# Spectral norms by chains of squarings: a scale at every third of 20 squarings instead of every second of 22, and two traces at the end

## The chip, the cores and the metric

The kernel runs on one core of one Trainium2 chip. The metric is the device time of one execution in microseconds (us). Before the change it is 1932.47 us, the median of 3 runs (1932.23 to 1932.93). The profiled execution spans 1930.8 us.

## The reference

The input x has 8 images of 512 channels and 1024 pixels, in f32. Four layers follow each other. Only the first has to do with the change:

```
f = relu(batchnorm(Wf x));  g = relu(batchnorm(Wg x));  h = Wh x     (64 channels each)
z = f^T g                                  per image, 1024 x 1024, of rank 64 at most
sigma = largest singular value of z        (S[:, 0] of an SVD)
x = Wv (z / sigma applied to h) + x
```

Layer 1 is a group norm with softmax attention over 1024 pixels, layer 2 an attention with 128 channels, layer 3 a product with the signs of a 512 x 512 weight matrix and an elementwise end.

The square of sigma is the largest eigenvalue of the 64 x 64 matrix (f f^T)(g g^T). The kernel never forms z. It squares this small matrix again and again, takes traces on the way to keep the numbers in range, and gets the logarithm of the eigenvalue as a weighted sum of the logarithms of the traces.

## The kernel before

**Layout.** Two images share one 128 x 128 matrix with two 64 x 64 blocks on the diagonal, so 8 images make 4 chains of squarings. For pair `j`, the tile `gm[j]` holds f f^T, g g^T and the product of h and g; it is made by `gram` (L1309, matmuls at L1312), from transposed tiles that `turn` (L1113, transposes at L1117) writes. `mask2` has ones in the two diagonal blocks; a matmul of it with a column sums that column within each image.

**A chain.** `chain(j, split)` (L995) is a generator: each `yield` hands control back, so that other work can be written between two steps. `products` (L1005) does one squaring: one matmul for the power and one for its transpose (L1008, L1009), both from the tile `cur`, which holds the two. `evict` (L1012) copies the results from PSUM to a new `cur`: with no scale, on ScalarE (L1022), or with `split` the first half on VectorE (L1024); with a scale on VectorE (L1030), or with `split` the second half on ScalarE (L1026). `diagonal` (L1033) multiplies with the identity and sums along each row (L1036, L1037), `total` (L1040) adds these row sums within an image by a matmul with one column (L1042) and copies the result to `tr` (L1043). The first trace is taken from f f^T and g g^T and divides the first product. Then come NSTEP = 11 rounds of two squarings. The second of a round is scaled by a power of the reciprocal of the trace taken a round earlier. After the last round there is a last trace; a logarithm (L1080), a weighted sum with the constants `quarters`, and an exponential (L1083) give 1 / sigma, which scales the matrix for the output (L1087). That makes 24 steps, 23 pairs of products and 12 totals in a chain.

**The first chain** (images 6 and 7, `split` on) stands in a block in which TensorE runs in the order of the program text (L1425). After each step of the chain the loop at L1428 writes a number of pieces of other work, taken from the generator `filler` (L1395): products of weights (L1265), Gram matrices (L1312), transposes (L1117), bias products (L1290), the scaling of z (L1173 to L1180). It also writes one `relu` (L1338), which runs on ScalarE. After the chain, `entering(0)` (L850) makes pv from the scaled matrix (L282) and the input of layer 1 of the first image (L403). What is left of `filler` comes after that.

**The other three chains** (`behind`, L1104) run inside the work of the first images: `fast` (L868) calls `chore(2)` after the pieces of the scores, the value weights and the values of layer 1, and every second call advances the chain by one step. The order of instructions there is set by the scheduler from the program text. Each engine then runs its instructions in that order. `entering` (L850) needs the chain of its pair to be finished.

**Buffers.** In the first part PSUM has two tiles of two banks (`wide`) and four of one bank (`bank`); products, totals, turns and bias products share the four. Later there are eight of one bank.

Of the kernel before, what the change touches and what calls it, by code (L numbers as in the profile page):

```python
# [8 lines left out]
F32 = mybir.dt.float32  # L9
F16 = mybir.dt.float16  # L10
I32 = mybir.dt.int32
AF = mybir.ActivationFunctionType
ALU = mybir.AluOpType
# [3 lines left out]
P = 128  # L17
# [47 lines left out]

NSTEP = 11

# [12 lines left out]
def kernel(  # L84
# [17 lines left out]
    nc = tc.nc  # L102
    mm = nc.tensor.matmul

    const = ctx.enter_context(tc.tile_pool(name="const", bufs=1))
# [4 lines left out]
    spin = ctx.enter_context(tc.tile_pool(name="spin", bufs=2))  # L110
# [10 lines left out]
    def bank():  # L121
        return psum["bank"].tile([P, HF], F32, tag="bank", name="bank")
# [17 lines left out]
    def half(i):  # L140
        return bass.ts(i, HF)

    def side(i):

        return slice(i * MID, (i + 1) * MID)
# [21 lines left out]
    ident = const.tile([P, P], F32, tag="ident", name="ident")  # L167
    make_identity(nc, ident)

    def block_ones(size, value, name):  # L170

        n = P // size
        member = const.tile([P, n], F32, tag=name + "_m", name=name + "_m")
        nc.vector.tensor_reduce(
            member, ident.rearrange("p (g j) -> p g j", j=size), AX.X, ALU.add
        )
        t = const.tile([P, n, size], F32, tag=name, name=name)
        nc.vector.tensor_scalar(
            t, member.unsqueeze(2).to_broadcast([P, n, size]), value, None, ALU.mult
        )  # L180
        return t.rearrange("p g j -> p (g j)")

    mask2 = block_ones(MID, 1.0, "mask2")
# [24 lines left out]
    minus_half = const.tile([P, CC], F32, tag="minus_half", name="minus_half")  # L208
    nc.gpsimd.memset(minus_half, -0.5)

    quarters = const.tile([P, NSTEP], F32, tag="quarters", name="quarters")
    for s in range(NSTEP):
        nc.gpsimd.memset(quarters[:, s : s + 1], 0.25**s)

    def vec(name):
        return ct[:, COL[name] : COL[name] + CC]
# [633 lines left out]
    def entering(n):  # L850

        b = order[n]
        f = load_f(b)

        def steps():
            while b // 2 not in ready:
                next(behind)
            if b % 2 == 0:
                for i in (b, b + 1):
                    pvs[i] = weights0(i)  # L860
            yield from enter(resident[b], f, pvs.pop(b))

        return steps()
# [131 lines left out]
    def chain(j, split):  # L995

        ff, gg, gh = (gm[j][:, i, :] for i in range(3))
        tr = spin.tile([P, NSTEP + 1], F32, tag="tr", name="tr")  # L1000

        def column(name):
            return spin.tile([P, 1], F32, tag=name, name=name)

        def products(a, at):  # L1005
            ps = [bank()] if not split else [bank(), bank()]
            pa, pb = ps[0][:, 0:P], ps[-1][:, 0:P] if split else ps[0][:, P : 2 * P]
            mm(out=pa, lhsT=at, rhs=a, start=True, stop=True)  # L1008
            mm(out=pb, lhsT=a, rhs=at, start=True, stop=True)  # L1009
            return ps[0], pa, pb  # L1010

        def evict(got, r=None, again=None, full=None):  # L1012

            both, pa, pb = got
            cur = spin.tile([P, 2, P], F32, tag="cur", name="cur")
            parts = [(cur[:, 0], pa), (cur[:, 1], pb)]
            if not split:
                parts = [(cur.rearrange("p i c -> p (i c)"), both[:, 0 : 2 * P])]
            for i, (dst, ps) in enumerate(parts):
                if r is None:  # L1020
                    if i or not split:
                        nc.scalar.copy(dst, ps)  # L1022
                    else:
                        nc.vector.tensor_copy(dst, ps)  # L1024
                elif i:
                    nc.scalar.activation(dst, ps, AF.Copy, scale=full)  # L1026
                elif again is None:
                    nc.vector.tensor_scalar(dst, ps, r, None, ALU.mult)
                else:
                    nc.vector.tensor_scalar(dst, ps, r, again, ALU.mult, ALU.mult)  # L1030
            return cur

        def diagonal(u, v):  # L1033
            d = spin.tile([P, P], F32, tag="diag", name="diag", bufs=1)
            t = column("tj")
            nc.vector.tensor_tensor(d, u, v, ALU.mult)  # L1036
            nc.vector.tensor_reduce(t, d, AX.X, ALU.add)  # L1037
            return t

        def total(t, s):  # L1040
            ps = bank()
            mm(out=ps[:, 0:1], lhsT=mask2, rhs=t, start=True, stop=True)  # L1042
            nc.vector.tensor_copy(tr[:, s : s + 1], ps[:, 0:1])  # L1043

        t = diagonal(ff, gg)
        got = products(gg, ff)
        total(t, 0)
        r = column("r")
        nc.vector.reciprocal(r, tr[:, 0:1])
        cur = evict(got, r, None, r)  # L1050
        yield

        root, half_ = column("root"), column("half_")
        nc.gpsimd.tensor_tensor(root, tr[:, 0:1], minus_half[:, 0:1], ALU.pow)
        nc.vector.tensor_tensor(half_, root, root, ALU.mult)
        nc.vector.tensor_tensor(half_, half_, tr[:, 0:1], ALU.mult)
        nc.vector.tensor_scalar(half_, half_, -0.5, 1.5, ALU.mult, ALU.add)
        nc.vector.tensor_tensor(root, root, half_, ALU.mult)
        t = None
        for s in range(1, NSTEP + 1):  # L1060
            cur = evict(products(cur[:, 0], cur[:, 1]))
            yield
            got = products(cur[:, 0], cur[:, 1])
            if t is None:
                cur = evict(got)
            else:
                total(t, s - 1)
                r, r2, r4 = column("r"), column("r2"), column("r4")
                nc.vector.reciprocal(r, tr[:, s - 1 : s])
                nc.vector.tensor_tensor(r2, r, r, ALU.mult)  # L1070
                if split:
                    nc.vector.tensor_tensor(r4, r2, r2, ALU.mult)
                cur = evict(got, r2, r2, r4)
            t = diagonal(cur[:, 0], ident)
            yield
        total(t, NSTEP)

        ln = spin.tile([P, NSTEP], F32, tag="ln", name="ln")
        rsig = column("rsig")
        nc.scalar.activation(ln, tr[:, 1:], AF.Ln)  # L1080
        nc.vector.tensor_tensor(ln, ln, quarters, ALU.mult)
        nc.vector.tensor_reduce(rsig, ln, AX.X, ALU.add)
        nc.scalar.activation(rsig, rsig, AF.Exp, scale=-0.125)  # L1083
        nc.vector.tensor_tensor(rsig, rsig, root, ALU.mult)
        for i in range(2):
            rr = side(i)
            nc.vector.tensor_scalar(  # L1087
                ff[rr, :].rearrange("p (i c) -> p i c", c=MID),
                gh[rr, rr].unsqueeze(1).to_broadcast([MID, 2, MID]),
                rsig[rr, :],  # L1090
                None,
                ALU.mult,
            )
        ready.add(j)
        yield
# [4 lines left out]
    def chains():  # L1100
        for j in rest:
            yield from chain(j, False)
# [109 lines left out]
    last = None  # L1212
    for b in range(B):
# [9 lines left out]
        def products(i, cc):  # L1223
            for h in range(NH):
                mm(  # L1225
                    out=banks[i][side(h), :],
                    lhsT=w0[i][:, cc, :],
                    rhs=xt[:, cc, half(h)],
                    start=cc == 0,
                    stop=cc == CC - 1,  # L1230
                )
# [22 lines left out]
        last = b, hraw  # L1254
# [83 lines left out]
    def relu(b, i):  # L1338
        t = (fs, gs)[i][b]
        nc.scalar.activation(t, t, AF.Relu, bias=bi0[:, i : i + 1], scale=sc0[:, i : i + 1])  # L1340
        if i == 0:
            nc.sync.dma_start(out=f_dram[b], in_=t)
# [10 lines left out]
    ps = bank()  # L1353
# [5 lines left out]
    ps = bank()  # L1359
# [65 lines left out]
    with tc.manual_schedule(engines={mybir.EngineType.PE}):  # L1425
        steps = entering(0)
        for k, _ in enumerate(chain(jl, True)):
            for _ in range(2 - k % 2 if k <= 2 * NSTEP else 4):  # L1428
                next(todo, None)
            for args in (next(relus, None),):  # L1430
                if args:
                    relu(*args)
        for k in range(CC + 2):
            next(steps)
            for _ in range(3 if k < CC else 5):
                next(todo, None)
        for _ in todo:
            pass
# [9 lines left out]
    with ExitStack() as main:  # L1448
# [5 lines left out]
        got = []  # L1454
# [177 lines left out]
```

## Time and profile before

| what | value |
|---|---|
| time, median of 3 | 1932.47 us |
| span of the profiled run | 1930.8 us |
| TensorE busy (matmuls) | 1906.6 us, 99% |
| weight loads of TensorE | 987.4 us, 51% |
| VectorE busy | 1158.2 us, 60% |
| ScalarE busy | 507.7 us, 26% |
| GpSimd busy | 229.7 us, 12% |
| granted TensorE clock | 0.998 |

PE in the profile is TensorE's matmuls, PEld its weight loads, DVE is VectorE, ACT ScalarE, POOL GpSimd. A line of the timeline gives the start and length in us, the engine, the line of the program, the operation, output<-inputs, and the number of records; in brackets, how long the engine stood idle before, and what ended that. One f32 matmul leaves two records of each kind. A length includes the time that a matmul takes to run through the array, so lengths of neighbours overlap, and what a matmul costs among others is read from start to start. The first chain begins at 114.1 us (matmuls that read gm). The other three lie between 225 and 758 us.

### The profile page before, as it was taken

How to read it: one execution, taken by the hardware profiler on the slowest of the kernel's cores; microseconds unless marked ns; L12 is line 12 of the kernel's file. 1: busy time of each engine (PE TensorE's matmuls, PEld its weight loads, DVE VectorE, ACT ScalarE, POOL GpSimd, SP SyncE). 2: the span in 40 equal slices, each digit the busy share in tenths (PEclk: the TensorE clock that was granted, in tenths of full speed). 3: DMA queues.
4: the chain of work that ended last, by engine and by line, in shares of the span. 5: the costliest groups of instructions: out<-in, count | busy, mean ns of one | idle time of the engine just before them, and what ended most of it. 6: DMA issues, size and time to landing. Idle time of an engine off the chain costs nothing.

```text
span 1930.8 us, 16673 instructions
## 1 busy us (share of the span) xinstructions
PE 1906.6 (99%) x6230; PEld 987.4 (51%) x6230; DVE 1158.2 (60%) x1875; ACT 507.7 (26%) x807; POOL 229.7 (12%) x178
## 2 busy tenths in 40 slices
PE   9999999999999999999999999999999999999997
PEld 4367456544655447454555446544645455544653
DVE  3256677448764687537754676348663775466647
ACT  2141222135222332025212331034202421143114
POOL 0000001200111001300121011201120011201121
PEclk9999999999999999999999999999999999999999
DMA  8420000002000120002000120002000200010001
GB/s 319 154 77 7 1 6 12 1 11 87 17 1 0 33 71 12 1 11 87 17 1 1 33 71 11 1 11 87 11 0 1 84 15 11 0 33 22 11 1 46
DMA packets 27784, 66.47 MB, mean 34 GB/s; under 512 B 4272, under 2 KB 5424, under 8 KB 27056
## 3 DMA queue, kind: packets, MB, share of 16 engines
q1 hardware_dynamic: 26768, 64.90, 10.0%
q8 instruction: 51, 0.84, 0.2%
q10 hardware_dynamic: 864, 0.43, 0.1%
q14 instruction: 37, 0.30, 0.1%
q0 software_dynamic: 64, 0.00, 0.0%
HBM read 38.51 MB, written 18.87 MB: 30 GB/s over the span
## 4 chain that ended last, share of the span: by engine, by line
PE 91%; DVE 7%; ACT 1%; issue 1%; DMA 0%; POOL 0%; DVEq 0%; ACTq 0%
PE bank L380 41%; PE bank L547 20%; PE bank L937 6%; PE bank L796 6%; PE bank L1225 4%; PE bank L648 3%; PE bank L403 2%; PE bank L665 2%; PE bank L1008 1%; PE wide L1265 1%; DVE both L739 1%; DVE both L709 1%; PE bank L1009 1%; PE wide L1312 1%; PE bank L688 1%; PE bank L817 1%
## 5 line engine op out<-in xcount | busy, mean ns | idle before, releaser
L547 PE MATMUL bank<-e,vt 128*128 128x512 f32 x768 | 334.0, 593 | 0.0
L547 PEld LDWEIGHTS bank<-e,vt 128*128 128x128 f32 x768 | 145.0, 190 | 175.4 <-issue 173.2
L380 PE MATMUL bank<-ut,h 128*128 128x512 f32 x384 | 181.3, 596 | 0.0
L337 DVE TENSOR_TENSOR e<-bank,e 128x512 f32<-128x512 f32 x128 | 87.6, 684 | 61.1 <-PE bank L380 60.3
L380 PE MATMUL bank<-us,hs 128*128 128x512 f32 x256 | 122.1, 599 | 1.3 <-DVE us L309 0.5
L380 PEld LDWEIGHTS bank<-ut,h 128*128 128x128 f32 x384 | 71.5, 190 | 85.8 <-issue 83.6
L937 PE MATMUL bank<-e,tpg 128*128 128x512 f32 x256 | 114.7, 595 | 0.0
L796 PE MATMUL bank<-tpg 128*128 128x512 f32 x256 | 114.6, 592 | 0.0
L803 ACT ACTIVATE e<-bank 128x512 f32<-128x512 f32 x128 | 76.5, 597 | 128.5 <-PE bank L796 128.5
L352 POOL TENSOR_TENSOR e<-e 128x512 f32<-128x512 f32 x32 | 44.1, 1378 | 419.5 <-ACT e L331 419.5
L380 PE MATMUL bank<-wo,h 128*128 128x256 f32 x384 | 91.8, 382 | 0.0
L808 DVE TENSOR_TENSOR esum<-esum,e 128x1024 f32<-128x1024 f32 x48 | 58.8, 1226 | 54.5 <-ACT e L803 54.5
L380 PE MATMUL bank<-h,wu 128*128 128x512 f32 x192 | 90.3, 593 | 0.7 <-ACT ut L342 0.7
L337 DVE TENSOR_TENSOR vt<-bank,vt 128x512 f32<-128x512 f32 x64 | 44.0, 688 | 70.5 <-PE bank L380 70.0
L937 PEld LDWEIGHTS bank<-e,tpg 128*128 128x128 f32 x256 | 48.1, 190 | 63.2 <-issue 63.1
L796 PEld LDWEIGHTS bank<-tpg 128*128 128x128 f32 x256 | 48.6, 190 | 60.8 <-issue 60.5
L352 POOL TENSOR_TENSOR ut<-ut 128x512 f32<-128x512 f32 x16 | 21.7, 1359 | 478.2 <-ACT ut L333 478.2
L380 PEld LDWEIGHTS bank<-wo,h 128*128 128x128 f32 x384 | 71.6, 190 | 13.5 <-ACT vt L331 4.1
L380 PEld LDWEIGHTS bank<-us,hs 128*128 128x128 f32 x256 | 46.7, 190 | 56.0 <-issue 46.4
L676 ACT ACTIVATE sg<-xt,rb 128x512 f16<-128x512 f32 x64 | 45.0, 718 | 103.7 <-DVE xt L667 100.2
L825 DVE RECIPROCAL rsum<-bank 128x512 f32<-128x512 f32 x15 | 50.3, 3356 | 28.6 <-PE bank L817 28.6
L1225 PE MATMUL bank<-xt,fg 128*64 128x512 f32 x256 | 59.7, 614 | 4.5 <-DMA fg<-in_w_fg 4.5
(325 smaller groups left out, 3090.1 us busy)
## 6 DMA issues: line engine op xcount, KB each, us to landing
xt<-in_x SPq DMA_DIRECT2D x55, 512.0 KB
out<-both SPq DMA_DIRECT2D x63, 256.0 KB
rfull<-rsum SPq DMA_DIRECT2D x60, 128.0 KB
f_dram<-f SPq DMA_DIRECT2D x8, 256.0 KB
fb<-f_dram SPq DMA_DIRECT2D x8, 256.0 KB
w<-in_w SPq DMA_DIRECT2D x1, 1024.0 KB
q<-in_w_q SPq DMA_DIRECT2D x1, 1024.0 KB
k<-in_w_k SPq DMA_DIRECT2D x1, 1024.0 KB
```

The source lines that it names most:

```text
L337: nc.vector.tensor_tensor(dst, ps, u, ALU.add)
L352: nc.gpsimd.tensor_tensor(c22, c22, c12, ALU.add)
L380: mm(out=ps[:, q * w : (q + 1) * w], lhsT=lt(ka, kb, q, k), rhs=rhs(ka, kb, q, k), start=first and q == 0 and k == 0, stop=last and k == 1 ...
L547: mm(out=ps, lhsT=a[:, t, bass.ts(r_, P)], rhs=e[t], start=first and t == 0, stop=last and t == NTH - 1, skip_group_check=True,)
L648: mm(out=ps[:, i, :], lhsT=xt[:, cc, bass.ts(4 * h + i, P)], rhs=sbw["tpg"][:, cc, 2 * P : 3 * P], start=cc == 0, stop=cc == CC - 1,)
L676: nc.scalar.activation(sg[:, cc, :], xt[:, cc, half(h)], AF.Sign, bias=rb3[:, cc : cc + 1])
L796: mm(out=ps, lhsT=pt[:, 0, bass.ts(t, P)], rhs=tt[:, 0, half(h)], start=True, stop=True,)
L803: nc.scalar.activation(e[:, half(h)], ps, AF.Exp, scale=float(P) ** -0.5)
L808: nc.vector.tensor_tensor(esum, esum, e, ALU.add)
L825: nc.vector.reciprocal(r, ps)
L937: mm(out=banks[h], lhsT=gt[:, t, :], rhs=es[t][:, half(h)], start=t == 0, stop=t == NT - 1,)
L1225: mm(out=banks[i][side(h), :], lhsT=w0[i][:, cc, :], rhs=xt[:, cc, half(h)], start=cc == 0, stop=cc == CC - 1,)
```

## The change

The number of squarings after the first product falls from 22 to 20, and a scale is applied at every third instead of every second. The chain starts with three squarings without a scale; then six rounds follow whose first squaring is scaled by the reciprocal of the trace of the round before, to the power that belongs to it; the last round has only two squarings. In place of a last power that is squared further, two traces are taken from the last one: the trace of the power, and the sum of the products of the power's and its transpose's elements, which is the trace of the power's square. The two bound the eigenvalue from both sides, and the mean of the logarithms of the bounds is a weighted sum of the traces' logarithms like the others; the constants `shares` replace `quarters`. The number of fillers after each step of the first chain follows the new pattern of steps. A chain now has 22 steps, 21 pairs of products and 8 totals, the last of which has two columns. It estimates the same 1 / sigma.

```diff
--- before.py
+++ after.py
@@ -65,7 +65,9 @@
-NSTEP = 11
+NSTEP = 6
@@ -208,9 +210,12 @@
     minus_half = const.tile([P, CC], F32, tag="minus_half", name="minus_half")
     nc.gpsimd.memset(minus_half, -0.5)
-    quarters = const.tile([P, NSTEP], F32, tag="quarters", name="quarters")
-    for s in range(NSTEP):
-        nc.gpsimd.memset(quarters[:, s : s + 1], 0.25**s)
+    shares = const.tile([P, NSTEP + 2], F32, tag="shares", name="shares")
+    last = 0.25 * 0.125**NSTEP
+    for s, share in enumerate(
+        [0.125 ** (s + 1) for s in range(NSTEP)] + [-0.5 * last, 0.75 * last]
+    ):
+        nc.gpsimd.memset(shares[:, s : s + 1], share)
     def vec(name):
         return ct[:, COL[name] : COL[name] + CC]
@@ -997,7 +1002,7 @@
         ff, gg, gh = (gm[j][:, i, :] for i in range(3))
-        tr = spin.tile([P, NSTEP + 1], F32, tag="tr", name="tr")
+        tr = spin.tile([P, NSTEP + 3], F32, tag="tr", name="tr")
         def column(name):
             return spin.tile([P, 1], F32, tag=name, name=name)
@@ -1030,19 +1035,18 @@
                     nc.vector.tensor_scalar(dst, ps, r, again, ALU.mult, ALU.mult)
             return cur
-        def diagonal(u, v):
+        def diagonal(u, v, t):
             d = spin.tile([P, P], F32, tag="diag", name="diag", bufs=1)
-            t = column("tj")
             nc.vector.tensor_tensor(d, u, v, ALU.mult)
             nc.vector.tensor_reduce(t, d, AX.X, ALU.add)
-            return t
-        def total(t, s):
+        def total(t, s, n=1):
             ps = bank()
-            mm(out=ps[:, 0:1], lhsT=mask2, rhs=t, start=True, stop=True)
-            nc.vector.tensor_copy(tr[:, s : s + 1], ps[:, 0:1])
-        t = diagonal(ff, gg)
+            mm(out=ps[:, 0:n], lhsT=mask2, rhs=t, start=True, stop=True)
+            nc.vector.tensor_copy(tr[:, s : s + n], ps[:, 0:n])
+        t = column("tj")
+        diagonal(ff, gg, t)
         got = products(gg, ff)
         total(t, 0)
         r = column("r")
@@ -1056,31 +1060,36 @@
         nc.vector.tensor_tensor(half_, half_, tr[:, 0:1], ALU.mult)
         nc.vector.tensor_scalar(half_, half_, -0.5, 1.5, ALU.mult, ALU.add)
         nc.vector.tensor_tensor(root, root, half_, ALU.mult)
-        t = None
-        for s in range(1, NSTEP + 1):
-            cur = evict(products(cur[:, 0], cur[:, 1]))
+        for s in range(NSTEP + 1):
+            got = products(cur[:, 0], cur[:, 1])
+            if s:
+                total(t, s)
+                r = column("r")
+                nc.vector.reciprocal(r, tr[:, s : s + 1])
+                if split:
+                    r2 = column("r2")
+                    nc.vector.tensor_tensor(r2, r, r, ALU.mult)
+                cur = evict(got, r, r, r2 if split else None)
+            else:
+                cur = evict(got)
             yield
-            got = products(cur[:, 0], cur[:, 1])
-            if t is None:
-                cur = evict(got)
-            else:
-                total(t, s - 1)
-                r, r2, r4 = column("r"), column("r2"), column("r4")
-                nc.vector.reciprocal(r, tr[:, s - 1 : s])
-                nc.vector.tensor_tensor(r2, r, r, ALU.mult)
-                if split:
-                    nc.vector.tensor_tensor(r4, r2, r2, ALU.mult)
-                cur = evict(got, r2, r2, r4)
-            t = diagonal(cur[:, 0], ident)
-            yield
-        total(t, NSTEP)
-        ln = spin.tile([P, NSTEP], F32, tag="ln", name="ln")
+            for more in range(2 if s < NSTEP else 1):
+                cur = evict(products(cur[:, 0], cur[:, 1]))
+                if more:
+                    t = column("tj")
+                    diagonal(cur[:, 0], ident, t)
+                yield
+        t = spin.tile([P, 2], F32, tag="td", name="td")
+        diagonal(cur[:, 0], ident, t[:, 0:1])
+        diagonal(cur[:, 0], cur[:, 1], t[:, 1:2])
+        total(t, NSTEP + 1, 2)
+        ln = spin.tile([P, NSTEP + 2], F32, tag="ln", name="ln")
         rsig = column("rsig")
         nc.scalar.activation(ln, tr[:, 1:], AF.Ln)
-        nc.vector.tensor_tensor(ln, ln, quarters, ALU.mult)
+        nc.vector.tensor_tensor(ln, ln, shares, ALU.mult)
         nc.vector.tensor_reduce(rsig, ln, AX.X, ALU.add)
-        nc.scalar.activation(rsig, rsig, AF.Exp, scale=-0.125)
+        nc.scalar.activation(rsig, rsig, AF.Exp, scale=-0.5)
         nc.vector.tensor_tensor(rsig, rsig, root, ALU.mult)
         for i in range(2):
             rr = side(i)
@@ -1425,7 +1434,8 @@
     with tc.manual_schedule(engines={mybir.EngineType.PE}):
         steps = entering(0)
         for k, _ in enumerate(chain(jl, True)):
-            for _ in range(2 - k % 2 if k <= 2 * NSTEP else 4):
+            for _ in range(4 if k == 3 * NSTEP + 3 else 2 if k != 1 and k % 3 < 2 else 1):
                 next(todo, None)
             for args in (next(relus, None),):
                 if args:
```

## The prediction

> **What bounds the kernel now.** I read the page's first part, then the busy time by stretches, then the timeline of TensorE in a late chain and at the end of the first one. The page:
>
> ```profile
> span 1930.8 us, 16673 instructions
> ...
> PE 1906.6 (99%) x6230; PEld 987.4 (51%) x6230; DVE 1158.2 (60%) x1875; ACT 507.7 (26%) x807; POOL 229.7 (12%) x178
> ```
>
> TensorE is busy for all but 24 us of the span, the next engine (VectorE) for 60%. But a busy share includes pipelining, so it doesn't prove that a removed matmul is removed time. The stretches do. Image boundaries by the chain that ended last (starts of its first value matmuls), columns: stretch, its length, busy us and records of each engine, clock, DMA:
>
> ```profile
> 312.82:538.57 225.75, 225.04 (x740) 119.39 (x740) 146.41 (x259) 63.32 (x104) 28.34 (x19) 1.00 0.08 25
> 538.57:761.69 223.12, 223.01 (x728) 118.31 (x728) 145.79 (x257) 63.29 (x105) 26.76 (x19) 1.00 0.08 25
> 761.69:973.54 211.85, 211.03 (x613) 105.31 (x613) 130.40 (x181) 57.50 (x88) 27.26 (x18) 1.00 0.08 27
> 973.54:1183.77 210.23, 209.72 (x610) 105.10 (x609) 127.62 (x175) 55.49 (x86) 27.09 (x18) 1.00 0.09 27
> ```
>
> The first two periods carry chains of squarings, the next two (and all after) don't. Two periods with chains last 448.87 us, two without 422.08: the chains cost 26.8 us there although they are fillers between big matmuls. They are paid in full on TensorE. How many there are, and what one costs in place (the records of the two lines of a product pair and of a total; two records are one f32 matmul, and 8 more of L1008 read gm at the chains' starts):
>
> ```profile
> L1008 PE MATMUL bank<-cur x176: 272/275/377, 116.8 to 753.8; 128*128 128x128 f32 x176
> ```
>
> ```profile
> L1042 PE MATMUL bank<-tj,mask x96: 167/250/271, 114.8 to 757.9; 128*128 128x1 f32 x96
> ```
>
> ```profile
> 258.05 1.88 PE L380 MATMUL bank<-us,hs 128*128 128x512 f32 x4
> 259.76 0.38 PE L1008 MATMUL bank<-cur 128*128 128x128 f32 x2
> 259.98 0.39 PE L1009 MATMUL bank<-cur 128*128 128x128 f32 x2
> 260.21 0.28 PE L1042 MATMUL bank<-tj,mask 128*128 128x1 f32 x2
> 260.35 1.96 PE L380 MATMUL bank<-ut,h 128*128 128x512 f32 x4
> ...
> 265.12 0.38 PE L1008 MATMUL bank<-cur 128*128 128x128 f32 x2
> 265.34 0.39 PE L1009 MATMUL bank<-cur 128*128 128x128 f32 x2
> 265.57 1.88 PE L380 MATMUL bank<-ut,hs 128*128 128x512 f32 x4
> ```
>
> 184/2 = 92 product pairs = 4 chains of 23; 48 totals = 4 of 12. From start to start, a pair takes 260.21 − 259.76 = 0.45 us, with no gap before it. A total takes 260.35 − 260.21 = 0.14, and the four records after a total need 0.08 more than after a pair (elsewhere 241.87 to 243.67 = 1.80 after a total, 243.67 to 245.39 = 1.72 without): 0.22 us in place. Check: the two periods hold 48 pairs and 27 totals, 48 × 0.45 + 27 × 0.22 = 27.5 us, against 26.8 measured, so 97% of such a sum is real.
>
> Last, the end of the first chain, which runs among small matmuls and where TensorE does wait:
>
> ```profile
> 158.31 0.39 PE L1008 MATMUL bank<-cur 128*128 128x128 f32 x2
> ...
> 158.53 0.39 PE L1009 MATMUL bank<-cur 128*128 128x128 f32 x2
> ...
> 159.15 1.09 PE L1117 MATMUL quad<-ident,g 128*128 128x128 f32 x8
> ...
> 160.08 1.06 PE L1312 MATMUL wide<-ft 128*128 128x128 f32 x8
> ...
> 161.57 0.35 PE L1042 MATMUL bank<-tj,mask 128*128 128x1 f32 x2 [0.43 <-DVE tj L1037]
> ```
>
> Eight such 128-column records stream in 0.90 us (0.1125 each), so L1312 was through at 160.98 and the last total stood 0.6 us for its diagonal, although two pieces of filler lay between.
>
> **What the Trainium skill says.** "TensorE: Matmul & The Clock Gate", Back-to-back issue gap: in a stream of weight loads and matmuls both set the spacing, about 81 ns at 128 columns. The principle holds, the number doesn't for f32 here: 112 ns a record; I use the trace's. "Perfetto Trace Analysis", Identifying the Most-Contended Engine: matmul busy share is no measure of the distance to the limit; hence the comparison of stretches above. "VectorE: DVE Perf Modes", the TRN2 errata: a small operation pays a fixed cost per instruction. The trace agrees: 128x1 operations take 0.16 us, 128x128 ones 0.29, so a dropped column operation is worth about 0.2 us of latency. "ScalarE: Activation LUTs", What ACT_TABLE_LOAD costs: 1283 ns a load; the trace has 1.28 us at 160.96 and again before the Exp. Two loads a chain before and after, so nothing changes.
>
> **The change part by part.**
> 1. *Squarings, 22 to 20.* Pairs per chain 23 to 21; two pairs × 0.45 = 0.90 us of TensorE a chain.
> 2. *Totals, 12 to 8* (the start, six scales, one of two columns at the end). Four × 0.22 = 0.88 us a chain. The two-column total is taken at the price of a one-column one: the built instruction list has one matmul for it, and weight loads bound it.
> So each chain sheds 1.78 us; three late chains 5.3 us (5.2 at 97%), the first 1.8.
> 3. *VectorE and ScalarE.* Diagonals fall from 12 to 9 a chain, scaled evictions from 11 to 7, plain ones on ScalarE rise from 12 to 14. All of that is beside TensorE in the late chains: chain steps come every 3.4 us or more (two 512-column products of 1.72) while an eviction takes 0.5. In all of 210 to 800 us the list of waits gives TensorE 1.1 us idle. I take zero, with +1 as the bad end: in the second image a scaled eviction now stands behind the 3.36 us reciprocal of the row sums (L825 group). The built order puts nine half-width products (3.9 us) before the next pair, against 3.4 + 0.2 + 0.2 + 0.5 us of VectorE work, so some 0.2 us may show.
> 4. *The late chains' last total* now needs two products and two reductions, 4 × 0.3 = 1.2 us on VectorE, in the same step. The built order puts 6.9, 3.0 and 3.4 us of other matmuls between the last pair and it. Nothing.
> 5. *The logarithms.* 8 columns instead of 11, 8 constants instead of 11: at 0.16 to 0.21 us fixed costs, nothing.
> 6. *The first chain's fillers* (the new count at L1428). Work is only moved: 34 + 4 pieces until the end instead of 35 + 4, the rest is drained after. What can differ is waiting. Before, by starts minus streaming time: 0.14 behind a 128x1024 copy on ScalarE, 0.9 at the scaling of z, 0.5 for a bank at the g turn, 2 × 0.5 where a scaled eviction met the bias products, 0.8 at the end: some 3.4 us. After, in the new order: step 2 has one filler (0.86 us) instead of two while ScalarE does two relus of 0.75, about 0.25; z about 0.3, since a pair and a total now lie between it and the next turn; g turn 0.5; the two bias encounters 0.2 each, because one column operation is gone from the path (no fourth power); and the end is worse. There only one filler (g turn, 0.9 us) lies between the last pair and the total, and in VectorE's built order are ft copy (0.69), eviction (0.29), diagonal and reduction, gt copy (0.69), second diagonal and reduction: the total can start about 3.0 us after the pair's start, TensorE has 0.45 + 0.9 for it, so it waits 1.65, not 0.8. Sum about 3.2. Bounds: if VectorE's copies fall better the end costs 0.9 (sum 2.4), if ScalarE is late too, 2.5 (sum 4.2). I take no change, range −1.0 to +1.0. The Ln and Exp after it stay covered by four fillers (3.6 us), as before: 161.57 to gm scaled at 164.8, and the weights of the next product at 165.5.
>
> Sum: 5.2 + 1.8 = 7.0 us. 1932.47 − 7.0 = **1925.5 us**.
>
> **The rivals.**
> - *The first chain gives its share back*: end wait at its bad bound and the moved fillers meeting full banks, +2 us. Speaks for it: one filler at the end. Against: fewer scales with fewer waits. 1932.5 − 5.2 + 0.2 = 1927.5.
> - *Removed work turns into waits.* If late steps were latency-bound, only half of the sum would show: 1929 to 1930. Against: 1.1 us of idle in 590 us, and the 97% check.
> - *Better than forecast*: waits at scales vanish with four fewer of them and the end is mild: −2 more, 1923.5.
> - *Slower*: each last total stands behind a 3.4 us reciprocal or a queue of 1.2 us sums on VectorE, and so do two scaled evictions: 3 × 3.4 + 2 = 12 lost, 7 won, 1937.5. The built order speaks against it, since three microseconds or more of matmuls stand ahead of each.
>
> **How the numbers follow.** Forecast 0.58, first chain gives back 0.20, waits 0.09, better 0.09, slower 0.04. The range 1923.3 to 1928.2 takes in the first three near cases and the better one. 0.2% is 3.9 us, so under 1928.6 is faster: 0.58 + 0.19 + 0.09 = 0.86; same 0.11; slower 0.03.
>
> **What would show it.** In the profile after: 168 − 8 records of L1008's line from cur and 64 of the total's; each late chain period shorter, the sum of late savings near 5.2; periods without chains equal to 0.1 us; the first chain from the gm pair to the weights of pv (114.1 to 165.5 before, 51.4 us) shorter by 1 to 3, with a wait of about 1.7 us before the two-column total. Wrong would be: new waits of TensorE on a chain's cur, or on td, of over 1 us in the late periods, or a longer first stretch.

## The result, and the profile after

The changed kernel takes 1924.77 us (median of 4 runs, 1924.53 to 1925.98) against 1932.57 us before: a ratio of 0.9961, 95% interval 0.9944 to 0.9978. The forecast was 1925.5 us, range 1923.3 to 1928.2. Measured again beside other kernels it was 1924.58 against 1932.18, ratio 0.9962 (0.9948 to 0.9975).

In the changed kernel some line numbers have moved: the pair is L1013 and L1014, the total L1045, the layer-1 products L385, the products with pv L408, the value matmuls L552. The first lines of its page:

```profile
span 1922.7 us, 16428 instructions
...
PE 1897.7 (99%) x6166; PEld 978.9 (51%) x6166; DVE 1136.0 (59%) x1761; ACT 509.5 (27%) x811; POOL 227.3 (12%) x175
```

TensorE lost 64 records and 8.9 us, the span 8.1. VectorE lost 22 us, which is more, but it was never the limit. The records of pairs and totals, from the two lines' own views:

```profile
L1013 PE MATMUL bank<-cur x160: 272/275/377, 115.7 to 723.9; 128*128 128x128 f32 x160
```

```profile
L1045 PE MATMUL bank<-tj,mask x56: 169/250/271, 113.6 to 719.9; 128*128 128x1 f32 x56
...
L1045 PE MATMUL bank<-td,mask x8: 168/251/272, 157.7 to 727.9; 128*128 128x2 f32 x8
```

84 pairs with the 8 records that read gm, and 32 totals, as counted ahead. The image periods, in the columns of before:

```profile
309.97:534.12 224.15, 223.73 (x729) 118.20 (x729) 144.35 (x245) 67.45 (x111) 26.93 (x20) 1.00 0.08 25
534.12:753.66 219.54, 219.32 (x696) 114.86 (x695) 137.79 (x215) 62.52 (x103) 26.13 (x18) 1.00 0.08 26
753.66:965.52 211.86, 211.04 (x614) 105.32 (x613) 128.18 (x176) 55.95 (x87) 27.24 (x18) 1.00 0.08 27
965.52:1175.76 210.24, 209.72 (x610) 105.11 (x609) 127.62 (x175) 55.48 (x86) 27.10 (x18) 1.00 0.09 27
```

The two with chains are 1.60 and 3.58 us shorter, the two without are the same to 0.01. So the time went where the chains are. In the second of the two the list of waits gives TensorE none, before or after, and the changed kernel has 5 pairs and 6 totals fewer there: 5 × 0.45 + 6 × 0.22 = 3.57 us by the forecast's prices, 3.58 measured.

For all the runs below I divide the span at the same four places, with the timeline and the chain that ended last: the *opening* up to the first matmul that reads gm; the *first stretch* from there to the first layer-1 product with wu (L380 before), which holds the first chain and all its fillers; the *late stretch* from there to the first value matmul of the third image, which holds the other three chains; and the *end*, from the end of the last arithmetic instruction to the end of the span. What lies between late stretch and end lasts 1164.5 us to 0.1, except in e1, where it is 1.0 longer.

| kernel | median us | opening | first stretch | late stretch | end |
|---|---|---|---|---|---|
| before | 1932.57 | 114.09 | 82.06 | 565.54 | 4.6 |
| after | 1924.77 | 112.89 | 79.46 | 561.31 | 4.5 |
| after, again (a1) | 1924.58 | 112.66 | 79.46 | 561.32 | 4.8 |
| e1, before with 20 squarings | 1929.34 | 112.61 | 80.74 | 562.86 | 4.6 |
| e7, first chain changed alone | 1929.63 | 112.75 | 79.46 | 565.56 | 4.5 |
| e2, late totals twice | 1928.98 | 113.59 | 79.45 | 564.03 | 4.6 |
| e4, late diagonals twice | 1927.05 | 113.67 | 79.46 | 561.88 | 5.9 |
| a2, the same again | 1926.71 | 113.26 | 79.46 | 561.90 | 5.8 |
| e3, one more filler at the end | 1924.54 | 112.77 | 79.40 | 561.30 | 4.7 |
| e8, the same with the order kept | 1924.52 | 112.57 | 78.63 | 561.31 | 4.5 |
| e5, 17 squarings | 1920.06 | 113.96 | 76.35 | 559.21 | 4.6 |
| e6, 11 squarings | 1905.91 | 113.62 | 72.30 | 549.27 | 4.4 |

The chains gave 82.06 − 79.46 = 2.60 us in the first stretch and 565.54 − 561.31 = 4.23 in the late one, 6.83 together; 7.0 were forecast, as 1.8 and 5.2. The late stretch gained less than the two periods together (1.60 + 3.58 = 5.18), which look like the 5.2 forecast: in the part ahead of them, from 196.15 to 312.82 before and from 192.35 to 309.97 after, the changed kernel is 0.95 us longer, although it has three totals fewer there and the same 21 pairs. The other 1.2 us between the two profiles lie in the opening, ahead of any changed matmul.

What takes the place of the wait that was shown at the first chain's end, from the timeline of after:

```profile
155.60 1.04 PE L1126 MATMUL quad<-ident,g 128*128 128x128 f32 x8
...
155.91 0.29 DVE L1040 TENSOR_TENSOR diag<-cur,ident 128x128 f32<-128x128 f32 x1
156.23 0.29 DVE L1041 TENSOR_REDUCE td<-diag 128x1 f32<-128x128 f32 x1
156.44 0.68 DVE L1132 COPY gt<-quad 128x512 f32<-128x512 f32 x1
...
157.03 0.28 DVE L1040 TENSOR_TENSOR diag<-cur 128x128 f32<-128x128 f32 x1
...
157.35 0.29 DVE L1041 TENSOR_REDUCE td<-diag 128x1 f32<-128x128 f32 x1
...
157.69 0.38 PE L1045 MATMUL bank<-td,mask 128*128 128x2 f32 x2 [1.05 <-DVE td L1041]
```

The filler's eight records (0.90) were through at 156.5; the total stood 1.2 us for two diagonals and, between them, the copy of a turn that sits ahead in VectorE's queue. The order was the expected one; the wait was 1.2 us instead of 1.65.

### The profile page after: what moved, and what is told of

It is laid out like the page before. It is cut to its first block, busy times and chain, and to the rows that moved or that the text cites. A ratio compares the mean times of both kernels' runs of the same rounds, so it can differ in the third digit from the quotient of the medians.

```text
span 1922.7 us, 16428 instructions
## 1 busy us (share of the span) xinstructions
PE 1897.7 (99%) x6166; PEld 978.9 (51%) x6166; DVE 1136.0 (59%) x1761; ACT 509.5 (27%) x811; POOL 227.3 (12%) x175
## 4 chain that ended last, share of the span: by engine, by line
PE 90%; DVE 8%; ACT 1%; issue 1%; DMA 0%; POOL 0%; DVEq 0%; ACTq 0%
PE bank L385 40%; PE bank L552 20%; PE bank L942 6%; PE bank L801 6%; PE bank L1234 4%; PE bank L653 3%; PE bank L408 2%; PE bank L670 2%; PE wide L1274 1%; DVE both L744 1%; DVE both L714 1%; PE wide L1321 1%; PE bank L1013 1%; PE bank L1014 1%; PE bank L693 1%
## 5 line engine op out<-in xcount | busy, mean ns | idle before, releaser
L552 PE MATMUL bank<-e,vt 128*128 128x512 f32 x768 | 333.8, 592 | 0.0
L552 PEld LDWEIGHTS bank<-e,vt 128*128 128x128 f32 x768 | 145.0, 190 | 175.4 <-issue 173.4
L385 PE MATMUL bank<-ut,h 128*128 128x512 f32 x384 | 181.5, 595 | 0.0
L385 PE MATMUL bank<-us,hs 128*128 128x512 f32 x256 | 121.9, 598 | 1.3 <-DVE us L314 0.5
L385 PEld LDWEIGHTS bank<-ut,h 128*128 128x128 f32 x384 | 71.3, 190 | 84.8 <-issue 83.3
L385 PE MATMUL bank<-wo,h 128*128 128x256 f32 x384 | 91.9, 382 | 0.0
L385 PE MATMUL bank<-h,wu 128*128 128x512 f32 x192 | 90.3, 593 | 0.7 <-ACT ut L347 0.7
L385 PEld LDWEIGHTS bank<-wo,h 128*128 128x128 f32 x384 | 71.6, 190 | 14.3 <-ACT vt L336 4.9
L385 PEld LDWEIGHTS bank<-us,hs 128*128 128x128 f32 x256 | 46.7, 190 | 56.1 <-issue 46.4
L653 PEld LDWEIGHTS bank<-tpg,xt 128*128 128x128 f32 x512 | 59.5, 192 | 7.2 <-issue 7.2
```

The source lines that it names most:

```text
L385: mm(out=ps[:, q * w : (q + 1) * w], lhsT=lt(ka, kb, q, k), rhs=rhs(ka, kb, q, k), start=first and q == 0 and k == 0, stop=last and k == 1 ...
L552: mm(out=ps, lhsT=a[:, t, bass.ts(r_, P)], rhs=e[t], start=first and t == 0, stop=last and t == NTH - 1, skip_group_check=True,)
L653: mm(out=ps[:, i, :], lhsT=xt[:, cc, bass.ts(4 * h + i, P)], rhs=sbw["tpg"][:, cc, 2 * P : 3 * P], start=cc == 0, stop=cc == CC - 1,)
```

## The experiments

**Are matmuls the price, and does each chain pay it?** e1 keeps the old pattern of scales and takes two squarings out.

```diff
-NSTEP = 11
+NSTEP = 10
```

> The kernel before with 10 rounds instead of 11: 20 squarings, 11 totals, a scale at every second squaring as before (two squarings fewer than the reference kernel before takes; the last trace stands for sigma). Theory (TensorE work is paid in full: 0.45 us a pair, 0.22 a total): 4 chains x (2 x 0.45 + 0.22) = 4.5 us less than before, about 1928.1. Rival A (the gain of the change comes from fewer scales, that is from shorter waits on VectorE, not from matmuls): one scale fewer of ten, under 1 us, about 1931.7. Rival B (only the pairs matter, totals are hidden): 3.6 us less and nearly all of the change's gain would have been the opening.

Measured: 1929.34 us against 1932.01 beside it, ratio to before 0.9986 (0.9979 to 0.9992): 2.7 us, where 4.5 were forecast. The first stretch is 1.32 shorter, the late one 2.68, together 4.0; its last image is 1.0 longer. There each engine runs the same lines in the same order, but one VectorE operation (L715 at 1913.85 us) takes 1.45 us instead of 0.55, while a GpSimd operation (L725) runs; whether that is the reason no run tests. Rival A (under 1 us) falls, and so does the idea that the pattern of scales made the gain: two squarings and a total less in each chain, without the new pattern, bring 4.0 of the 6.8. The late stretch has one new wait of 0.5 us (a row sum, L817), and 2.68 + 0.5 = 3.2 is near the 3.3 that three chains × 1.12 × 0.97 should give. Rival B's price for the late chains, 3 × 0.9 = 2.7, would fit only without that wait; e2 decides between them.

e7 changes the first chain alone; the late ones call the old function.

```diff
         for j in rest:
-            yield from chain(j, False)
+            yield from chain_old(j, False)
```

> The change in the first chain alone; the three late chains as before (22 squarings, a scale at every second). Theory (each chain sheds 1.78 us of TensorE, the first chain's waits stay what they were in sum): 1.8 less than before, about 1930.2 to 1930.8, and the stretch between the first chain's start and the last late chain's image 1.6 to 1.8 shorter. Rival (the first chain gives its share back through the wait before the two-column total): no change against before. Rival (the first chain held most of the gain): 4 or more.

Measured: 1929.63, ratio 0.9987 (0.9980 to 0.9993). First stretch 79.46, the same as in the whole change to 0.01; late stretch 565.56, the same as before to 0.02. So the late chains don't feel the first one, and the change splits cleanly: the first chain's part is 2.6 us, not 1.8, and the late part is 4.2, not 5.2. The total was forecast well, its division wasn't. The next runs look for both errors.

**The price of a total.** e2 takes each inner total of the late chains twice.

```diff
             if s:
-                total(t, s)
+                for _ in range(1 if split else 2):
+                    total(t, s)
```

> The changed kernel with each of the six inner totals of the three late chains taken twice (the same sum again, the same result): 18 more one-column matmuls and copies. Theory (0.22 us a total in place, of which 0.08 falls on the matmul after it): +4.0 us, about 1928.8. Rival (a total costs only its own start-to-start time of 0.14): +2.5. Rival (totals are hidden beside the big matmuls): 0.

Measured: 1928.98, late stretch +2.72 us for 18 totals. Taken alone that is 0.15 each, the rival's number. But the list of what TensorE waited for from 200 us until the third image says more. After:

```profile
PE bank L1013 <- DVE cur L1035: 0.7, 1, 0.7
PE bank L385 <- DVE us L314: 0.5, 1, 0.5
PE bank L1013 <- DVE r_e L235: 0.5, 1, 0.5
PE bank L408 <- ACT pv L292: 0.3, 1, 0.3
```

and with the totals twice:

```profile
PE bank L385 <- DVE us L314: 0.5, 1, 0.5
PE bank L408 <- ACT pv L292: 0.3, 1, 0.3
```

Two waits of a pair on a scaled eviction, 0.66 and 0.47 us by the timeline, are gone (for the second the list names r_e, which ended just after the eviction). 2.72 + 1.13 = 3.85, or 0.21 a total, if the vanished waits are added back. The run also has a stretch without waits, which needs no such sum: the second of the two periods with chains, here to be compared with 534.12:753.66 of after.

```profile
536.20:757.07 220.87, 220.65 (x707) 116.20 (x707) 138.44 (x221) 62.49 (x103) 26.13 (x18) 1.00 0.08 25
```

Six totals more make it 220.87 − 219.54 = 1.33 us longer, 0.22 each: the price stands. That the median met its forecast of 1928.8 is luck: only 2.7 of the 4.4 us over after (1924.58) lie in the chains, and e2's time is 2.85 us longer than its profiled span, where after's is 1.9.

Why did the waits go? The timeline of e2 at the place of the first:

```profile
255.38 1.88 PE L385 MATMUL bank<-us,hs 128*128 128x512 f32 x4
...
257.10 1.02 PE L385 MATMUL bank<-ut,h 128*128 128x512 f32 x2
...
257.29 0.54 DVE L1035 TENSOR_SCALAR cur<-bank,r 128x256 f32<-128x256 f32 x1
...
257.96 0.42 PE L1013 MATMUL bank<-cur 128*128 128x128 f32 x2
```

The eviction comes no earlier, 4.1 us after the start of the total instead of 3.9. The scheduler, which sets the order from the text, has put the pair behind one large matmul more (L385 x2, 0.86 us from start to start), and at the second place behind three more of half the width.

**Where the late gain went short.** In before the same list holds 0.5, 0.3 and 0.3 us, 1.1 in all; after it holds 2.0. The 0.9 is about what was lost: 5.2 − 0.9 = 4.3 against 4.23 measured. The larger wait, from the timeline of after:

```profile
252.31 0.28 PE L1045 MATMUL bank<-tj,mask 128*128 128x1 f32 x2
...
252.76 1.40 DVE L417 SCALAR_TENSOR_TENSOR xt<-bank,bvo,xt 128x512 f32<-128x512 f32 x2
...
254.08 1.27 DVE L420 BATCH_NORM_STATS2 st<-xt 128x6 f32<-128x512 f32 x2
...
255.27 0.14 DVE L1046 COPY tr<-bank 128x1 f32<-128x1 f32 x1
...
256.19 0.54 DVE L1035 TENSOR_SCALAR cur<-bank,r 128x256 f32<-128x256 f32 x1
...
256.79 0.49 PE L1013 MATMUL bank<-cur 128*128 128x128 f32 x2 [0.66 <-DVE cur L1035]
```

The total is done by 252.6. Its copy, of 0.14 us, runs at 255.27: four operations of layer 1's input stand ahead of it on VectorE. Reciprocal and scaled eviction follow, and the next pair, 5 us after the one before (251.76), finds its operand 0.66 us late. From start to start the wait costs a little more: the four records of L385 at 254.25 last 2.54 us until the pair, instead of 1.72. The other wait (284.23) has the same form, with sums of 1.2 us and the rsqrt of the group norm in the queue. In before, other steps of the chain fell on this place. As e2 shows, the order on TensorE has its part in it too: a pair that stands one large or three half-width matmuls later doesn't wait. No run makes that change alone. e4 asks from the other side whether VectorE matters: it doubles the late diagonals.

```diff
                 if more:
-                    t = column("tj")
-                    diagonal(cur[:, 0], ident, t)
+                    for _ in range(1 if split else 2):
+                        t = column("tj")
+                        diagonal(cur[:, 0], ident, t)
```

> The changed kernel with each of the six inner diagonals of the three late chains taken twice on VectorE (a product with the identity and a row sum, the same result): 36 more small operations, some 11 us of VectorE. Theory (VectorE stands beside TensorE in the late images): no change, within 0.5 us of the changed kernel. Rival (part of the gain is VectorE's relief, 22 us less busy than before): some 4 us slower, half of the gain given back.

Measured: 1927.05, 2.5 us over the changed kernel, which looks like the rival. The stretches say otherwise: first stretch the same, late stretch +0.57 for 9.4 us of added VectorE work, and the rest in opening and end, where no diagonal runs. The 0.57 is a net: the wait of 0.66 is gone, since here too the pair stands behind one large matmul more, and two waits of a total for its diagonal have come:

```profile
PE bank L1045 <- DVE tj L1041: 0.9, 2, 0.8
```

I ran it again unedited to see whether opening and end belong to it.

> The changed kernel with the late diagonals taken twice, unedited from the run before. There the time was 2.4 us over the changed kernel, but the stretch with the chains only 0.6 longer; the opening was 0.8 and the end after the last instruction 1.3 longer. Theory (opening and end are set by transfers and differ from one execution or build to another, for reasons other than VectorE): the stretch with the chains again 0.5 to 0.7 longer than in the changed kernel, opening and end anywhere. Rival (they belong to this program): opening 113.7 and end 5.9 again, each within 0.2.

Measured: 1926.71; late stretch 561.90, +0.59; opening 113.26, not 113.67; end 5.8, again over 1 us longer than in the others. So each theory had one half: the opening moves from execution to execution, the longer end belongs to this program. The net effect of the added VectorE work is 0.6 us, so the rival's 4 us falls and the relief of 22 us is worth little; but where a small operation falls in VectorE's queue costs half a microsecond and more at a time. What lengthens the end of this program I can't say; it lies after the last arithmetic instruction.

**Where the first chain's extra 0.8 came from.** e3 puts a second piece of filler into the hole before the two-column total.

```diff
-            for _ in range(4 if k == 3 * NSTEP + 3 else 2 if k != 1 and k % 3 < 2 else 1):
+            for _ in range(4 if k == 3 * NSTEP + 3 else 2 if k == 3 * NSTEP + 2 or (k != 1 and k % 3 < 2) else 1):
```

> The changed kernel with two pieces of other work instead of one between the last pair of the first chain and its two-column total; the piece is taken from those that are drained after the chain. Theory (the 1.05 us wait before that total is a real hole that 0.9 us of moved work fills): the wait falls to 0.2 or less, 0.9 us less, about 1923.9, and the stretch from the first pair to the weights of pv gets no longer. Rival (the hole is refilled elsewhere: the chain's end moves later and the weights of pv or the first bank of layer 1 wait instead): no change.

Measured: 1924.54, first stretch 79.40 instead of 79.46: nothing. The wait before the total did fall to 0.15. My theory fell and the rival held, but not where it looked for it. In the timeline of e3 after the weights of pv:

```profile
165.41 1.04 PE L1126 MATMUL quad<-ident,f 128*128 128x128 f32 x8
...
166.28 1.07 PE L1126 MATMUL quad<-ident,g 128*128 128x128 f32 x8
...
167.28 1.92 PE L408 MATMUL bank<-fb,pv 64*128 64x512 f32 x4
...
168.08 0.29 PEld L408 LDWEIGHTS bank<-fb,pv 64*128 64x128 f32 x2 [0.51 <-DVE ft L1132]
```

and in that of after:

```profile
166.43 1.04 PE L1126 MATMUL quad<-ident,f 128*128 128x128 f32 x8
...
167.39 1.13 PE L408 MATMUL bank<-fb,pv 64*128 64x512 f32 x4
...
168.45 1.09 PE L1126 MATMUL quad<-ident,g 128*128 128x128 f32 x8
```

The four records of L408 need 1.13 us where they run freely and 1.92 in e3: both turns of the next pair come just ahead, take the four PSUM banks, and the second product waits for a copy of a turn. Before the change it was the same (1.92 at 171.26). In after, three groups of filler stand between the products with pv in another phase, since one piece fewer was used up by the chain: one turn comes ahead of L408 and one behind it, and the wait of 0.8 is gone. e3 moves the phase back. e8 fills the hole and keeps the phase: two pieces before the total, three after.

```diff
-            for _ in range(4 if k == 3 * NSTEP + 3 else 2 if k != 1 and k % 3 < 2 else 1):
+            for _ in range(3 if k == 3 * NSTEP + 3 else 2 if k == 3 * NSTEP + 2 or (k != 1 and k % 3 < 2) else 1):
```

> The changed kernel with two pieces before the two-column total and three instead of four after it, so that the pieces drained after the chain stay the same ones in the same places. Theory (moving a piece out of the drained part brought back a 0.8 us wait for a PSUM bank at the first layer-1 products, because both turns of a pair then came together; that is where the filled hole went): here that wait stays away, the hole of 0.9 closes, and the three pieces (2.7 us) no longer cover the 3.3 us from the total to the scaled matrix, so about 0.4 is lost before the weights of pv: the stretch until the weights of layer 1 is 0.4 to 0.5 shorter than in the changed kernel. Rival (the hole is time that cannot be had): 0, or longer.

Measured: 1924.52; first stretch 78.63, 0.83 us shorter than in after. The mechanism holds. The size was larger than forecast: the wait for the scaled matrix did come, but shortened the one for pv behind it from 0.67 to 0.29. The gain of 0.8 doesn't show in the medians (1924.52 against 1924.58). The profiled execution was the fastest of five, 1923.31; the others have no profile, so where the rest went isn't shown.

**The change, unedited, again**, for what is not the chains:

> The changed kernel again, unedited. What stands to be seen is the part of its time that has nothing to do with the chains: between the first profile of before and of after, the opening until the first chain (input transfers) differed by 1.2 us with the same instructions. Theory (1.2 us of the gain was the chance of one execution's transfers; the chains give 6.8): over many executions some 6.8 to 7.8 below before, 1924.5 to 1925.5, and the opening of this profile anywhere from 112.5 to 114.1. Rival (the opening belongs to the program): 112.9 again within 0.2.

Measured: 1924.58, inside the theory's 1924.5 to 1925.5. First and late stretch agree with the first profile to 0.01 us; the opening is 112.66, 0.23 from 112.89, just outside the rival's 0.2. Over the twelve profiles of this case it lies between 112.57 and 114.09, and before's profile was the longest; before's median over 46 other executions is 1932.01, 0.7 below that of the profiled execution (1932.7). The difference is made in the first 25 us, among products that read x as it comes in: the first transposes (of the tile hraw) begin at 24.84 us in before and at 23.65 in after. So more than half of the 1.2 us, 0.7, was the chance of that execution. Between 6.83 in the chains and 7.6 in the medians some 0.7 us stay open.

**How far it goes.** e5 and e6 cut further, with more fillers a step so that no piece is missing when the chain ends.

```diff
-NSTEP = 6
+NSTEP = 5
...
-            for _ in range(4 if k == 3 * NSTEP + 3 else 2 if k != 1 and k % 3 < 2 else 1):
+            for _ in range(4 if k == 3 * NSTEP + 3 else 2):
```

> The changed kernel with five scaled rounds instead of six: 17 squarings, 7 totals, 18 pairs a chain, and two fillers after every step of the first chain (three squarings fewer stand for the same sigma). Theory (linear in pairs and totals): 4 x (3 x 0.45 + 0.22) = 6.3 less, and up to 1.0 less for the waits of the first chain that the second fillers cover: 1917.5 to 1918.5. Rival (what is left of the chains hides better once they are shorter, or their first step's fixed costs dominate): less than 4 us.

Measured: 1920.06, ratio to before 0.9936 (0.9922 to 0.9950). 1917.5 to 1918.5 were forecast, so the gain fell short. The first stretch is 3.1 shorter than in after: 1.57 are matmuls by the price list, TensorE's idle time ahead of matmuls falls by 0.9, and 0.6 I can't place. The late stretch is 2.1 shorter instead of 4.6: its waits rise from 2.0 to 3.5 us, among them 0.9 of a total on its diagonal, and some 1.0 stays unexplained.

> The changed kernel with three scaled rounds: 11 squarings, 5 totals, 12 pairs a chain, three fillers after every step of the first chain and four after its last. Theory: 4 x (9 x 0.45 + 3 x 0.22) = 18.8 less, and up to 1.5 for waits: 1904.5 to 1906. Rival (three chains end so early that their image's other waits come up): under 15 us less, over 1910.

Its edit is NSTEP = 3, three pieces a step and four after the last. Measured: 1905.91, ratio 0.9865 (0.9849 to 0.9880). First and late stretch together are 19.2 us shorter than in after, where 18.8 and up to 1.5 were forecast: 7.2 in the first stretch and 12.0 in the late one, where waits come to 3.4 us instead of 2.0, one of them 1.6. So the line in pairs and totals holds in the sum over half of the chain; in the parts it doesn't, with 4.7 and up to 1.5 forecast for the first stretch and 14.1 for the late one. The second of the two late periods, which has no chain left here, follows the prices: 18 pairs and 7 totals less are 9.6 us, 9.3 came, with one new wait of 0.4. It is the fastest of these kernels, 26 us below before. The two bounds whose mean it takes then lie within ln(8)/2048 of each other in the logarithm of the eigenvalue.

## Why the prediction was right, point by point

- **TensorE pays in full.** Right, and the ground of the rest: periods without chains are unchanged, the second late period follows the price list in after, e2 and e6, and 6.83 us came of 7.0.
- **Points 1 and 2, the counts and prices** (0.45 a pair, 0.22 a total): right. e2 gives 0.22 a total where no wait is in the way, and 3.58 us came where 3.57 are priced; e1's late stretch fits within 0.1 with its new wait added back. The check in the forecast counts one total too many: the two periods hold 26, not 27, so it gives 27.3 us and 98%.
- **Point 3, "I take zero" for VectorE in the late chains: wrong.** It was the step that failed. Two scaled evictions came late by 0.66 and 0.47 us, where before had one of 0.3. The late gain was 4.23, not 5.2. (That the two periods named as the check add to 5.18 is chance; the loss lies ahead of them.) The bad end of +1 that I gave it was hit, but not at the reciprocal that I named: it was the input of layer 1 and the group norm in the first image. I had compared VectorE's operations with the time between chain steps, 3.4 us, and not asked how long the queue ahead of a 0.14 us copy is. It was 2.7 us. Nor had I asked how many large matmuls the scheduler would leave between the total and the next pair.
- **Point 4, the late last totals**: right, none waits.
- **Point 5**: right; the logarithm takes 0.21 us as before, and two table loads of 1.28 us stand around it.
- **Point 6, the first chain's fillers**: its sum was right for the stretch I had summed: 51.44 us from the gm pair to pv's weights became 48.79, that is 1.78 of matmuls and 0.9 for the piece that is now drained later; waits were equal in sum. In parts, the wait at the end was 1.2 instead of 1.65. "Work is only moved" was wrong: the piece cost nothing where it went, because it changed the phase of the fillers against the products with pv, and a 0.8 us wait for a bank vanished. I had not looked behind the chain's end.
- So the forecast's total owes something to luck, to two errors of 0.8 and 1.0 us with opposite signs; each is within the range I gave for it, but neither was foreseen. The rivals fell: the first chain didn't give its share back (e7), the late ones gave back 1 us of 5.2 and not half of it, and nothing of 12 us came on VectorE.

## What to carry to other kernels

On an engine that is busy without gaps, price a removed instruction from start to start in its real neighbourhood, including what it does to the next one, and check the price on two stretches with and without it; where no wait came in between, this held to 1%. Then look for waits in the queues of the other engines: compare not durations but how much stands ahead of the small operation that the busy engine needs, and how much work the busy engine has until it needs the result. An experiment that lets a scheduler run again can move both, so read the order around a wait before saying what removed it. And a piece of work moved elsewhere also moves the phase of everything behind it; when an obvious hole is filled and nothing comes of it, look for the wait that came back.

## What the runs showed of the hardware that I had not expected

- First and late stretch repeat to 0.02 us from profile to profile and from build to build, where the instructions are the same, and what follows up to the end to 0.1. The times of 46 executions of before scatter over 2 us; in the profiled ones such differences lie in opening, end and the time outside the span.
- The opening varied by 1.5 us over twelve profiles, the end was 4.4 to 4.8 us in nine of the ten programs and 5.8 and 5.9 in both runs of the tenth, and the time outside the span was 2.85 us in e2 and 1.5 to 2.0 in the others. Effects under 2 us should be read from stretches, not from medians.
- A copy of 0.14 us that stood behind four operations on VectorE, an engine that is 59% busy, started 2.7 us after its input and cost TensorE 0.66 us of idle time; with one large matmul (0.86 us) more ahead of the pair the wait was gone.
